# Two attention pipelines: VectorE and ScalarE issued in the written order of the steps, with the steps cut anew

## The chip, the cores and the metric

The program runs on one core of a Trainium2 chip. The metric is the device time of one execution in microseconds (us), as the median of ten runs. A core has five engines that run side by side and wait for one another through semaphores: TensorE (matmuls and transposes; PE in the profile, with its weight loads apart as PEld), VectorE (DVE), ScalarE (ACT), GpSimd (POOL) and SyncE (SP, which here only starts DMAs). Matmul results land in PSUM, a small memory of eight banks per partition; everything else is in SBUF.

## The reference, cut to what matters

The reference is a two-layer decoder over 16 samples of 256 tokens with 256 features, and a context of 120 tokens per sample. Each sublayer is `x = x + f(layernorm(x))`:

- layer 0: causal self-attention with rotary positions (16 heads of 16), cross-attention to the context, and a feed-forward part that picks 10 of 16384 experts for each of 8 heads;
- layer 1: self-attention with a small band added to the scores, a cross-attention whose result is joined as `[c, c2q, c*c2q, c*q2c]` and multiplied by one matrix, and a mixture of 8 experts of which each token uses two.

What the change touches are the two stretches of attention: both attentions of layer 0, and the band attention of layer 1 with the cross-attention and the routing that follow it.

## The kernel before, in words

All 16 samples of `x` stay in SBUF (`xt`), and each stage updates them in place. There are four stretches of time: (1) self- and cross-attention of layer 0 as one pipeline over 32 units (16 samples of the first layer, then 16 of the second); (2) the many-expert part; (3) the band attention of layer 1, beside which the "flow" of each finished sample runs (cross-attention and routing); (4) the mixture of experts, over tiles of 256 tokens.

**The pipeline.** An `Attention` layer has six stages for a unit: `prepare` (layernorm and projections), `ready` (transposed keys and queries), `maxima` (the scores once, for the maximum of each row), `weigh` (the scores again with the maximum in them, and Exp), `values` and `finish`. `run` makes one visit per `v`, and in visit `v` stage `i` works on unit `v - i`. The stages are generators, and each `yield` ends a step. `maxima` and `weigh` go in pairs: at each of their yields they hand out a list of matmuls and a function `after` with what has to be done to the result. `run` issues the two lists in turns, then both `after` functions, then some steps of the other stages (`others_go`: 2 for each pair in the self-attention, 3 in the cross-attention and in stretch 3), then the next pair. A self-attention visit has six pairs, a cross-attention visit four, a band visit eight. The scores of `maxima` have one PSUM buffer (`sa`), so the matmuls of the next pair can't start before VectorE has reduced the last one; the scores of `weigh` have one too (`sb`), which ScalarE empties with Exp. The small results of all other steps go through two rings of two PSUM banks, `t1` and `t2`.

**The order within a visit.** The other stages take turns through `turns`: the first step of `prepare`, the first of `ready`, of `values`, of `finish`, then the second of each, and so on. A visit begins with two of these steps, so TensorE's first work in a visit is the first step of `prepare`. In stretch 3 a second generator, `side`, alternates with them. It begins a new flow in each visit and gives each live flow one step in each of 7 rounds, the older flow first. A flow has 15 steps.

**The layernorm.** `fresh` gives the normalized sample. For the first of each four samples it first takes the statistics of all four (eight tiles, each one BN_STATS and one BN_AGGR on VectorE, lines 119 and 120), the root on ScalarE (line 122), and the reciprocal on VectorE (123). Then, for every sample, `normalized` computes `xn` on VectorE (line 108), and `transposed` turns it on TensorE (131) and copies it to SBUF on ScalarE (132). These last three are in one step. A flow calls `fresh` for its own sample alone, and takes statistics a second time before the routing (lines 1053 to 1057).

**What sets the order of instructions.** In `run` only TensorE stands under `tc.manual_schedule`: its instructions are issued in the order in which the program writes them. For VectorE, ScalarE and GpSimd a scheduler decides at compile time: it goes by the program's order too, but takes a later instruction first where its model finds the earlier one not ready. At run time each engine keeps to the list that came out. ScalarE's functions need tables: a change between the square root and Exp shows as an instruction ACT_TABLE_LOAD.

Lines to follow in the code: `xn` 108; statistics 119 to 123; `run` 165 to 192; maxima 293 (without a mask) and 297, 307 to 309 (causal); Exp 335; the flow 949 to 1158, with its `both` at 1018, its result `y` at 1043, the routing at 1078 to 1137; `side` 1163 to 1171.

Of the kernel before, what the change touches and what calls it, by code (L numbers as in the profile page):

```python
# [13 lines left out]
AF = mybir.ActivationFunctionType  # L14
ALU = mybir.AluOpType
AX = mybir.AxisListType
PSUM = bass.MemoryType.PSUM

P = 128
D = 256  # L20
# [31 lines left out]
def tile_decoder(ctx: ExitStack, tc: tile.TileContext, a: dict, out: bass.AP, last: int = 4):  # L52
    nc = tc.nc
    B = a["x"].shape[0]
# [15 lines left out]
    xt = []  # L70
# [12 lines left out]
    eps = T(cst, [P, 1], "eps")  # L83
    nc.vector.memset(eps, EPS)
    mv = T(cst, [P, NT, 2], "mv")
    rstd = T(cst, [P, NT], "rstd")

    def col(c, n=1):
# [4 lines left out]


    def layernorm_stats(wk):
        for i in range(NT):
            st = T(wk, [P, 6], "bnst")
            nc.vector.bn_stats(st, xt[i // 2][:, i % 2, :])
            nc.vector.bn_aggr(mv[:, i, :], st)
        std = T(wk, [P, NT], "std")  # L100
        nc.scalar.activation(std, mv[:, :, 1], AF.Sqrt, bias=eps)
        nc.vector.reciprocal(rstd, std)

    def normalized(wk, b):
        xn = T(wk, [P, 2, D], "xn")
# [4 lines left out]
            )  # L110
        return xn

    def fresh(wk, b, group=4):

        if b % group == 0:
            ts = range(2 * b, 2 * (b + group))
            for i in ts:
                st = T(wk, [P, 6], "bnst")
                nc.vector.bn_stats(st, xt[i // 2][:, i % 2, :])
                nc.vector.bn_aggr(mv[:, i, :], st)  # L120
            std = T(wk, [P, 2 * group], "std")
            nc.scalar.activation(std, mv[:, ts.start : ts.stop, 1], AF.Sqrt, bias=eps)
            nc.vector.reciprocal(rstd[:, ts.start : ts.stop], std)
        return normalized(wk, b)

    def transposed(ps, xn, dst):

# [30 lines left out]
    def run(stages, n, gap, joint=(2, 3), side=None, more=0):  # L158

        with tc.manual_schedule(engines={mybir.EngineType.PE}):
            for v in range(n + len(stages) - 1 + more):
                going = {i: stage(v - i) for i, stage in enumerate(stages) if 0 <= v - i < n}
                pairs = [going.pop(i) for i in joint if i in going]
                others = deque([turns(going.values())] + ([] if side is None else [side(v)]))

                def others_go(k):
                    while k and others:
                        g = others.popleft()
                        if next(g, 0) is None:
                            others.append(g)
                            k -= 1

                def advance():
                    held = []
                    for g in pairs:  # L180
                        step = next(g, 0)
                        while step is None:
                            others_go(1)
                            step = next(g, 0)
                        if step != 0:
                            held.append(step)
                    return held

                others_go(2)
                held = advance()  # L190
                while held:
                    others_go(gap(v))
                    for pair in zip_longest(*(mms for mms, _ in held)):
                        for mm in pair:
                            if mm is not None:
                                mm()
                    for _, after in held:
                        after()
                    held = advance()
                others_go(-1)  # L200
# [245 lines left out]
    with ExitStack() as st:  # L446
# [21 lines left out]
        half = DH // 2  # L468

        def self_prepare(b, c):  # L470
            xnT = T(wk, [P, 2, S], "xnT")
            transposed(ps, fresh(wk, b), xnT)
            yield
            k, q, v = c["k"], c["q"], c["v"] = ks[b % 2], qs[b % 4], vs[b % 5]
            for t in range(2):
                ts = slice(t * P, (t + 1) * P)
                pp = T(ps, [P, 2 * NH, 2, half], "t1")
                project_rows(pp.rearrange("p h s d -> p (h s d)"), xnT, ts, wa, 0, 2 * D)
                ra = T(wk, [P, 2 * NH, 2, half], "ra", bufs=1)
# [26 lines left out]
            nc.scalar.copy(v[:, :, :, 0:DH], pv.rearrange("p t (h d) -> p t h d", h=NH))  # L506
            yield
# [4 lines left out]
        def cross_prepare(b, c):  # L512
            cT = T(wk, [P, 2, NQ], "cT")
            nc.sync.dma_start(cT, a["ctxT"][b].rearrange("(c p) q -> p c q", p=P))
            xnT = T(wk, [P, 2, S], "xnT")
            transposed(ps, fresh(wk, b), xnT)
            yield
            q, v = c["q"], c["v"] = qs[(b + B) % 4], vs[(b + B) % 5]
            pq = T(ps, [P, 2, D], "t1")
# [325 lines left out]
    with ExitStack() as st:  # L845
# [16 lines left out]
        ps2 = pool(s6, "sc4", 1, PSUM)  # L862

        def band_prepare(b, c):
            c["xnT"] = T(wk4, [P, 2, S], "xnT", bufs=4)
            transposed(ps, fresh(wk4, b), c["xnT"])
            yield

        def band_ready(b, c):
# [78 lines left out]
        def flow(b):  # L948
            load(b)
            cx, cT = context.pop(b)  # L950
            xn = fresh(wk, b, 1)
            nc.gpsimd.tensor_tensor(xt[b], xt[b], badd.unsqueeze(1).to_broadcast([P, 2, D]), ALU.add)

            qc = T(wk, [P, 2, NQ], "qc")
# [20 lines left out]
            for t in range(2):  # L975
                nc.scalar.activation(
                    e[:, t], p_s[:, t], AF.Exp, bias=nm[:, t : t + 1], accum_out=z[:, t : t + 1]
                )
            nc.vector.reciprocal(z, z)
            for t in range(2):  # L980
                nc.scalar.activation(e[:, t], e[:, t], AF.Copy, scale=z[:, t : t + 1])
            yield

            pm = T(ps, [1, 2, P], "t1")
            for t in range(2):
# [3 lines left out]
            be = T(wk, [1, 2, P], "be", bufs=1)  # L989
            bz = T(wk, [1, 1], "bz")  # L990
            nc.scalar.activation(be, pm, AF.Exp, bias=low, scale=-1.0, accum_out=bz)
            nc.vector.reciprocal(bz, bz)
            yield
            pt = T(ps, [NQ, 2, P], "t1")
            for t in range(2):
                nc.tensor.transpose(pt[:, t, :], e[:, t], ident)
# [32 lines left out]
                    )  # L1029
            q2c = T(wk, [P, 2], "q2c")  # L1030
            nc.scalar.copy(q2c, pd)

            wb = T(wk, [P, 2, D], "wb", bufs=1)
            for dc in range(2):
                nc.vector.scalar_tensor_tensor(
                    wb[:, dc, :], wl[:, 6 + dc, :], q2c[:, dc : dc + 1], wl[:, dc, :], ALU.mult, ALU.add
                )
            yield
            parts = [(u, w, c) for u, w in ((att, wl[:, 2:4]), (both, wl[:, 4:6]), (xnT, wb)) for c in range(2)]
            for t in range(2):  # L1040
                y = T(ps, [P, D], "t2")
# [4 lines left out]
                nc.vector.tensor_add(xt[b][:, t, :], xt[b][:, t, :], y)  # L1046
                if t == 0:
                    yield
            xr = T(wk, [P, 2, RW], "xr")
            ts = slice(2 * b, 2 * b + 2)  # L1050
            for t in range(2):
                stats = T(wk, [P, 6], "bnst")
                nc.vector.bn_stats(stats, xt[b][:, t, :])
                nc.vector.bn_aggr(mv[:, 2 * b + t, :], stats)
            std = T(wk, [P, 2], "std2")
            nc.scalar.activation(std, mv[:, ts, 1], AF.Sqrt, bias=eps)
            nc.vector.reciprocal(rstd[:, ts], std)
            shift = T(wk, [P, 2], "shift")
            nc.vector.scalar_tensor_tensor(shift, mv[:, ts, 0], -1.0, rstd[:, ts], ALU.mult, ALU.mult)
            for t in range(2):  # L1060
# [17 lines left out]
            nc.vector.tensor_reduce(red, pl, AX.X, ALU.max)  # L1078
            nc.vector.tensor_tensor(rw, pl, over(red), ALU.subtract)
            nc.scalar.activation(rw, rw, AF.Exp)  # L1080
            nc.vector.tensor_reduce(red, rw, AX.X, ALU.add)
            nc.vector.reciprocal(red, red)
            nc.vector.tensor_tensor(rw, rw, over(red), ALU.mult)
# [51 lines left out]
            for t in range(2):  # L1135
                for k in range(2):
# [5 lines left out]
                    )  # L1142
                    tc.declare_no_dep(ins.ins, group="rows", reason="no two tokens have one place")
                    tc.add_to_no_dep_group("rows", ins.ins)
            yield

            pt = T(ps, [NE, 2, P], "t1")
            for t in range(2):
# [13 lines left out]
        def side(v):  # L1162
            b = v - len(layer.stages())
            if 0 <= b < B:
                flows.append(flow(b))
            for _ in range(7):
                for g in list(flows):
                    if next(g, 0) is None:
                        yield
                    else:  # L1170
                        flows.remove(g)
# [247 lines left out]
```

## Time and profile before

| What | Value |
|---|---|
| median of 10 runs | 3883.72 us (3875.56 to 3890.93) |
| the profiled execution | 3893.37 us, its span 3891.7 us |
| stretch 1, both attentions of layer 0 | from the start to about 752 us |
| stretch 2, many experts | to about 2317 us |
| stretch 3, band attention, flows and routing | to about 3300 us |
| stretch 4, mixture of experts | to the end |
| ScalarE's table loads in stretch 1 at lines 122 and 335 | 5 and 5 |
| table loads from 2290 to 3300 us at lines 335, 122, 1056 | 27, 17 and 16, of 1283 ns each |

The profile names an operation by the line of the program, the engine and the tiles that it writes and reads. "PE sa<-kT,qT" is the score matmul of `maxima`, "DVE q<-sa" its reduction. The answers by time stretch give busy microseconds and, behind them, the clock that was granted to TensorE as a share of full speed. In a list of instructions in order of time, a bracket says how long the engine had been idle before the line and which instruction ended that.

### The profile page before, as it was taken

To read this page: it belongs to the slowest core of one execution; us is meant where nothing else is said; L and a number is where in the kernel's file an instruction comes from. 1 tells how busy PE (TensorE), PEld (TensorE's weight loads), DVE (VectorE), ACT (ScalarE), POOL (GpSimd) and SP (SyncE) were. 2 spreads that over 40 slices of the span, in tenths; PEclk is the share of its full clock that TensorE was granted. 3 is DMA by queue.
4 is the path that set the end of the run, shared out by engine and by line. 5 is a ranking of instruction groups with operands and counts; after the bars stand their busy time and mean duration, and the time that the engine had idled before them with its cause. 6 is when DMAs were issued, how large, how long until landed. Compare 5 with 4: busy or idle time off the path is not lost.

```text
span 3891.7 us, 131086 instructions
## 1 busy us (share of the span) xinstructions
PE 3468.0 (89%) x57482; PEld 2887.7 (74%) x57482; DVE 2295.4 (59%) x9263; ACT 1648.3 (42%) x2873; POOL 1625.9 (42%) x1611
## 2 busy tenths in 40 slices
PE   6999999659999999999999997888888886999999
PEld 4666788458888888888888885666666665788887
DVE  6777543498888888888888733444344433111111
ACT  2555566334444444444444323555454432233222
POOL 2333200036666666666666652333233321333332
PEclk8999999869999999999999997899898866999999
DMA  9200000200000000000000010000000001566564
GB/s 333 92 2 2 5 9 8 94 3 4 4 4 4 4 4 4 4 4 4 4 4 4 4 33 1 4 20 21 17 23 18 22 21 55 170 187 186 172 184 133
DMA packets 49327, 182.01 MB, mean 47 GB/s; under 512 B 14889, under 2 KB 36785, under 8 KB 42354
## 3 DMA queue, kind: packets, MB, share of 16 engines
q1 hardware_dynamic: 29840, 144.22, 10.5%
q0 software_dynamic: 18048, 29.14, 3.6%
q8 instruction: 451, 7.39, 0.8%
q14 instruction: 122, 1.00, 0.1%
q10 hardware_dynamic: 866, 0.26, 0.0%
HBM read 150.66 MB, written 57.15 MB: 53 GB/s over the span
## 4 chain that ended last, share of the span: by engine, by line
PE 67%; DVE 22%; ACT 5%; POOL 3%; issue 2%; DMA 0%; another core or an unknown queue 0%; POOLq 0%; DVEq 0%; ACTq 0%
PE acc L784 9%; PE t L145 7%; PE h L137 7%; PE hid L137 7%; PE y L1283 7%; PE sa L263 6%; DVE hot L740 5%; PE t L759 5%; PE t L368 4%; POOL hot L747 2%; PE t L1043 2%; PE t L137 2%; DVE q L293 2%; PE t L245 2%; PE sb L263 2%
## 5 line engine op out<-in xcount | busy, mean ns | idle before, releaser
L747 POOL TENSOR_TENSOR hot<-hot,w 104x1024 f32<-104x1024 f32 x256 | 523.4, 2045 | 281.4 <-DVE hot L740 177.3
L740 DVE TENSOR_TENSOR hot<-wij,iota 104x1024 f32<-104x1024 f32 x512 | 598.7, 1211 | 61.8 <-ACT w L730 54.0
L137 PE MATMUL hid<-xnT,w_dn 128*128 128x128 f32 x4096 | 522.2, 281 | 3.6 <-issue 2.0
L137 PEld LDWEIGHTS hid<-xnT,w_dn 128*128 128x128 f32 x4096 | 482.7, 193 | 15.2 <-issue 3.4
L784 PE MATMUL acc<-w_up,hg 128*128 128x256 f32 x2048 | 482.1, 381 | 0.0
L263 PE MATMUL sa<-kT,qT 32*128 32x256 f32 (+2 forms) x3072 | 382.2, 371 | 110.1 <-DVE q L293 80.6
L778 POOL TENSOR_TENSOR hg<-hg,gate 128x512 f32<-128x512 f32 x256 | 342.6, 1338 | 255.4 <-ACT hg L777 245.9
L759 PEld LDWEIGHTS t<-hot,hot 104*32 104x32 f32 x32768 | 310.4, 110 | 162.4 <-POOL hot L747 108.7
L759 PE MATMUL t<-hot,hot 104*32 104x32 f32 x32768 | 341.3, 199 | 94.7 <-POOL hot L747 83.8
L335 ACT ACTIVATE pT<-sb 128x1024 f32<-128x1024 f32 (+1 forms) x288 | 295.2, 1025 | 285.2 <-PE sb L263 223.7
L263 PEld LDWEIGHTS sa<-kT,qT 32*128 32x128 f32 x3072 | 257.0, 200 | 201.9 <-DVE q L293 113.2
L784 PEld LDWEIGHTS acc<-w_up,hg 128*128 128x128 f32 x2048 | 371.9, 190 | 42.6
L263 PE MATMUL sb<-qmT,kT 32*128 32x256 f32 (+2 forms) x2560 | 370.0, 412 | 15.2 <-ACT pT L335 15.1
L766 ACT COPY gate<-t 128x512 f32<-128x512 f32 x256 | 271.0, 1058 | 253.2 <-PE t L759 253.0
L293 DVE TENSOR_REDUCE q<-sa 128x4 f32<-128x1024 f32 (+1 forms) x192 | 230.7, 1202 | 182.4 <-PE sb L263 103.1
L346 POOL TENSOR_TENSOR pT<-pT,bandf 128x260 f32<-128x260 f32 x256 | 184.6, 743 | 324.2 <-ACT pT L335 322.1
L137 PE MATMUL h<-xT,wt 128*128 128x256 f32 x1248 | 279.5, 382 | 6.0 <-ACT xT L1274 6.0
L777 ACT ACTIVATE hg<-hid 128x512 f32<-128x512 f32 x256 | 153.7, 601 | 306.1 <-PE hid L137 304.8
L1283 PE MATMUL y<-wt,hT 128*128 128x256 f32 x1248 | 275.7, 379 | 0.0
L137 PEld LDWEIGHTS h<-xT,wt 128*128 128x128 f32 x1248 | 223.9, 190 | 55.3 <-ACT xT L1274 10.8
L1292 POOL DMA_INDIRECT out_y<-ys,toi x78 | 123.4, 1581 | 337.1 <-DVE ys L1291 302.6
L1283 PEld LDWEIGHTS y<-wt,hT 128*128 128x128 f32 x1248 | 237.1, 190 | 32.2
(289 smaller groups left out, 5931.6 us busy)
## 6 DMA issues: line engine op xcount, KB each, us to landing
wt<-in_m_w SPq DMA_DIRECT2D x39, 2052.0 KB, 8.6
rows<-in_zeros SPq DMA_DIRECT2D x32, 1040.0 KB, 28.4
x<-in_x SPq DMA_DIRECT2D x16, 256.0 KB, 4.5
w_dn<-in_p_dn SPq DMA_DIRECT2D x2, 2048.0 KB
w_up<-in_p_up SPq DMA_DIRECT2D x1, 4096.0 KB, 23.6
out_y<-x SPq DMA_DIRECT2D x16, 256.0 KB, 2.1
cT<-in_ctxT SPq DMA_DIRECT2D x32, 120.0 KB, 2.1
cx<-in_ctx SPq DMA_DIRECT2D x16, 120.0 KB, 2.3
```

Of the source, the lines that this page charges most:

```text
L137: nc.tensor.matmul(o, lhsT=w[:, dc, c0 : c0 + n], rhs=rhs[:, dc, :], start=dc == 0, stop=stop and dc == 1)
L145: nc.tensor.matmul(o, lhsT=xT[:, dc, tok], rhs=w[:, dc, c0 : c0 + n], start=bias is None and dc == 0, stop=dc == 1)
L263: nc.tensor.matmul(sc[0 : ls.stop - ls.start, r, g, 0 : rs.stop - rs.start], lhsT=lhs[rows_, g0 + g, ls], rhs=rhs[rows_, g0 + g, rs], star ...
L293: nc.vector.tensor_reduce(to, sc[:, :, :, 0:nk], AX.X, ALU.max)
L335: nc.scalar.activation(pT[0:kn], sc[0:kn], AF.Exp, scale=1.0 / math.sqrt(DH))
L740: nc.vector.tensor_tensor(t, wij[:, k, cs].unsqueeze(2).to_broadcast([HS, NC, PK]), iota[0:HS].unsqueeze(1).to_broadcast([HS, NC, PK]), AL ...
L747: nc.gpsimd.tensor_tensor(hot[1], hot[1], w[:, cs].unsqueeze(2).to_broadcast([HS, NC, PK]), ALU.mult)
L759: nc.tensor.matmul(pg[q * NLO : (q + 1) * NLO, t, :], lhsT=hi[:, t, i0 : i0 + NLO], rhs=hj[:, t, j0 : j0 + NLO], start=True, stop=True,)
L766: nc.scalar.copy(gate[:, :, c * NC : (c + 1) * NC].rearrange("p l t -> p t l"), pg)
L778: nc.gpsimd.tensor_tensor(hg, hg, gate[:, s * L : (s + 1) * L, :], ALU.mult)
L784: nc.tensor.matmul(acc, lhsT=hg[:, i, :], rhs=w_up[:, l, :], start=l == 0, stop=l == NLO - 1)
L1283: nc.tensor.matmul(y, lhsT=hT[:, fc, h * P : (h + 1) * P], rhs=w2[:, fc, :], start=fc == 0, stop=fc == FF // P - 1,)
```

## The change

Five things are done. First, in `run` VectorE and ScalarE join TensorE in the written order. Second, `fresh` becomes a generator: at the first of a group of samples it issues statistics and the root, yields, and issues the reciprocal in the next step; `normalized` is then called by its user, in the same step as `transposed`. Third, the flow's steps are cut differently: the yields stand behind an instruction on ScalarE (or another engine) whose result VectorE reads next. The flow has 17 steps in place of 15. Fourth, `side` gives nine rounds in a visit in place of seven, so that a flow lives for two visits and not for three. Fifth, `std` is one tile for the whole program. No arithmetic is added or dropped.

```diff
+IN_ORDER = {mybir.EngineType.PE, mybir.EngineType.DVE, mybir.EngineType.Activation}
...
+    def stats(wk, b, n=1):
+        ts = slice(2 * b, 2 * (b + n))
+        for i in range(ts.start, ts.stop):
+            st = T(wk, [P, 6], "bnst")
+            nc.vector.bn_stats(st, xt[i // 2][:, i % 2, :])
+            nc.vector.bn_aggr(mv[:, i, :], st)
+        nc.scalar.activation(std[:, ts], mv[:, ts, 1], AF.Sqrt, bias=eps)
+
+    def rstds(b, n=1):
+        nc.vector.reciprocal(rstd[:, 2 * b : 2 * (b + n)], std[:, 2 * b : 2 * (b + n)])
+
     def fresh(wk, b, group=4):
         if b % group == 0:
...
-        return normalized(wk, b)
+            stats(wk, b, group)
+            yield
+            rstds(b, group)
...
-        with tc.manual_schedule(engines={mybir.EngineType.PE}):
+        with tc.manual_schedule(engines=IN_ORDER):
...
         def self_prepare(b, c):
+            yield from fresh(wk, b)
             xnT = T(wk, [P, 2, S], "xnT")
-            transposed(ps, fresh(wk, b), xnT)
+            transposed(ps, normalized(wk, b), xnT)
             yield
...
         def flow(b):
             load(b)
             cx, cT = context.pop(b)
-            xn = fresh(wk, b, 1)
+            yield from fresh(wk, b, 1)
+            xn = normalized(wk, b)
...
                     e[:, t], p_s[:, t], AF.Exp, bias=nm[:, t : t + 1], accum_out=z[:, t : t + 1]
                 )
+            yield
             nc.vector.reciprocal(z, z)
             for t in range(2):
                 nc.scalar.activation(e[:, t], e[:, t], AF.Copy, scale=z[:, t : t + 1])
-            yield
...
             nc.scalar.activation(be, pm, AF.Exp, bias=low, scale=-1.0, accum_out=bz)
+            yield
             nc.vector.reciprocal(bz, bz)
-            yield
...
             nc.scalar.copy(q2c, pd)
+            yield
             wb = T(wk, [P, 2, D], "wb", bufs=1)
...
-            yield
             parts = [(u, w, c) for u, w in ((att, wl[:, 2:4]), (both, wl[:, 4:6]), (xnT, wb)) for c in range(2)]
...
                 if t == 0:
                     yield
+            stats(wk, b)
+            yield
+            rstds(b)
...
             nc.scalar.activation(rw, rw, AF.Exp)
+            yield
             nc.vector.tensor_reduce(red, rw, AX.X, ALU.add)
...
                     tc.add_to_no_dep_group("rows", ins.ins)
-            yield
             pt = T(ps, [NE, 2, P], "t1")
...
-            for _ in range(7):
+            for _ in range(9):
```

`cross_prepare` and `band_prepare` change as `self_prepare` does.

More of the change, by code (lines that the diff above doesn't have):

```diff
@@ L85, in tile_decoder @@
     mv = T(cst, [P, NT, 2], "mv")
+    std = T(cst, [P, NT], "std")
     rstd = T(cst, [P, NT], "rstd")
@@ L95, in layernorm_stats @@
     def layernorm_stats(wk):
[L96 to L102, printed above, removed]
+        stats(wk, 0, B)
+        rstds(0, B)
     def normalized(wk, b):
@@ L111, in normalized @@
         return xn
+    def stats(wk, b, n=1):
[7 more added lines that the diff above has]
+        nc.vector.reciprocal(rstd[:, 2 * b : 2 * (b + n)], std[:, 2 * b : 2 * (b + n)])
     def fresh(wk, b, group=4):
         if b % group == 0:
[L116 to L123, printed above, removed]
-        return normalized(wk, b)
+            stats(wk, b, group)
+            yield
+            rstds(b, group)
     def transposed(ps, xn, dst):
@@ L514, in cross_prepare @@
             nc.sync.dma_start(cT, a["ctxT"][b].rearrange("(c p) q -> p c q", p=P))
+            yield from fresh(wk, b)
             xnT = T(wk, [P, 2, S], "xnT")
-            transposed(ps, fresh(wk, b), xnT)
+            transposed(ps, normalized(wk, b), xnT)
             yield
@@ L864, in band_prepare @@
         def band_prepare(b, c):
+            yield from fresh(wk4, b)
             c["xnT"] = T(wk4, [P, 2, S], "xnT", bufs=4)
-            transposed(ps, fresh(wk4, b), c["xnT"])
+            transposed(ps, normalized(wk4, b), c["xnT"])
             yield
@@ L1048, in flow @@
                     yield
+            stats(wk, b)
+            yield
+            rstds(b)
             xr = T(wk, [P, 2, RW], "xr")
             ts = slice(2 * b, 2 * b + 2)
[L1051 to L1057, printed above, removed]
             shift = T(wk, [P, 2], "shift")
```

## The prediction

> **What bounds the kernel now.** I read the page first, then busy time and granted clock by stretches, then the instructions in order of time where one visit ends and the next begins, then TensorE's waits.
>
> ```profile
> PE 3468.0 (89%) x57482; PEld 2887.7 (74%) x57482; DVE 2295.4 (59%) x9263; ACT 1648.3 (42%) x2873; POOL 1625.9 (42%) x1611
> PE   6999999659999999999999997888888886999999
> PEclk8999999869999999999999997899898866999999
> ```
>
> TensorE bounds every stretch. The change touches slices 1 to 8 (stretch 1) and 24 to 33 (stretch 3); the second group has the idle time and the low clock. By stretches (busy us, and after POOL the clock):
>
> ```profile
> 100.00:400.00 300.00, 273.06 (x3533) 197.51 (x3532) 229.90 (x529) 155.31 (x228) 96.90 (x137) 0.99 0.08 28
> 500.00:700.00 200.00, 194.14 (x2614) 166.24 (x2612) 81.99 (x134) 130.75 (x269) 13.02 (x19) 1.00 0.03 8
> 2609.00:3051.70 442.70, 384.44 (x3365) 289.85 (x3365) 197.60 (x559) 221.85 (x410) 149.72 (x206) 0.90 0.06 20
> ```
>
> Self- and cross-attention leave 9% and 3% of TensorE idle, at full clock. The third line is eight visits of the band (from one square-root table load of line 122, at 2609.07 us, to the eighth after it, at 3051.7): 55.3 us each, of which 58.3 / 8 = 7.3 us idle, and 10% of the busy time, 4.8 us, lost to the clock. What little there is to win is there. TensorE's waits from 2460 to 3180 us say on whom:
>
> ```profile
> PE sa L263 <- DVE q L293: 43.6, 27, 3.6
> PE t L1149 <- ACT batt L1004: 14.3, 6, 3.1
> PE sb L263 <- ACT pT L335: 10.2, 11, 1.1
> PE t L1111 <- DVE either L1102: 8.0, 10, 0.9
> ```
>
> The lines that decide are those of a visit's end. In the self-attention, TensorE:
>
> ```profile
> 265.81 0.37 PE L263 MATMUL sb<-qmT,kT 32*128 32x256 f32 x1
> 266.11 0.65 PE L131 MATMUL t<-ident,xn 128*128 128x128 f32 x4
> 266.60 0.60 PE L245 MATMUL t<-ident,k 128*128 128x128 f32 x4
> 267.83 0.66 PE L245 MATMUL t<-ident,q 128*128 128x128 f32 x4 [0.62 <-ACT xnT L132]
> ```
>
> and VectorE:
>
> ```profile
> 266.23 0.76 DVE L297 TENSOR_TENSOR own<-sa,causal 128x256 f32<-128x256 f32 x2
> ...
> 267.50 0.68 DVE L308 TENSOR_REDUCE m<-own 128x4 f32<-128x512 f32 x1
> 268.09 0.40 DVE L108 TENSOR_SCALAR xn<-x,mv,rstd 128x256 f32<-128x256 f32 x1
> ```
>
> The last score matmul ends at 266.2, and line 131 follows without a gap: it turns an `xn` that VectorE made a visit earlier. The `xn` at 268.09 belongs to the next visit's sample. VectorE runs ahead, because the scheduler let it. In the cross-attention it is the same: line 131 starts at 552.14, right behind the scores, while VectorE reduces them until 553.4 and only then makes the next `xn`:
>
> ```profile
> 552.34 1.16 DVE L293 TENSOR_REDUCE q<-sa 128x8 f32<-128x960 f32 x1 [1.34 <-PE sa L263]
> 553.41 0.73 DVE L108 TENSOR_SCALAR xn<-x,mv,rstd 128x256 f32<-128x256 f32 x2
> ```
>
> **What the change does to the head of a visit.** `normalized` and `transposed` stay in one step, and it is the first of the visit. In the written order `xn` stands behind the reduction of the last pair, and TensorE, in the same order, has nothing in front of line 131. So the run-ahead is lost.
>
> Self-attention, samples that don't begin a group: the maximum's chain takes VectorE to 268.3, two `xn` (0.73) to 269.1, and line 131 starts there in place of 266.11: 3.0 us. It absorbs the 0.62 us wait for `xnT` shown above (the Exp before it on ScalarE is then over). Net 2.4 us. Visits 3, 5 to 7, 9 to 11, 13 to 15, 17 and 18: 12 x 2.4 = 29 us.
>
> Cross-attention: 553.41 + 0.73 + 0.05 - 552.14 = 2.05 us. Visits 19, 21 to 23, 25 to 27, 29 to 31: 10 x 2.05 = 20.5 us. What queues behind line 131 on TensorE (line 137, 1.9 us) can't cover it, for it comes later in the order.
>
> **Groups.** At the first of four samples the first step is eight statistics, and ScalarE's root behind them stops everything that follows on ScalarE. At the end of stretch 1 the same pair of instructions comes every 0.68 us:
>
> ```profile
> 752.04 0.43 DVE L98 BATCH_NORM_STATS2 bnst<-x 128x6 f32<-128x256 f32 x1
> 752.51 0.18 DVE L99 BATCH_NORM_AGGREGATE mv<-bnst 128x2 f32<-128x6 f32 x1
> 752.72 0.43 DVE L98 BATCH_NORM_STATS2 bnst<-x 128x6 f32<-128x256 f32 x1
> ```
>
> Eight are 5.4 us. Counted from 266.2: maximum to 268.3, statistics to 273.7, root (0.30) to 274.05, then the copy of `kT` (0.59) that frees a `t1` bank, 274.65. TensorE has the turned keys, the first turned queries and the sums (0.5 + 0.5 + 1.5) and is out of work at 268.7: 6.0 us. Today the four groups of the self-attention take their statistics before 28 us, beside the load of `x`, so visits 4, 8 and 12 pay all of it: 18 us. For the cross-attention the same count gives 6.0 at visit 16 and 4.4 at 20, 24 and 28 (shorter maximum, 1.9 us of line 137 as cover): 19.2. Today's four cost 2.24, 2.24, 2.5 and 1.4 us of TensorE (the stalls behind the loads at 213, 313, 407 and 494): +10.8. At the start the first copy of `xnT` no longer stands behind the fourth root (27.20): TensorE begins at 26.7 and not at 28.13, -1.4.
>
> Waits in stretch 1: 29 + 20.5 + 18 + 10.8 - 1.4 = +77 us.
>
> **The clock.** One of today's stalls, in order of time,
>
> ```profile
> 218.18 1.05 PE L245 MATMUL t<-ident,q 128*128 128x128 f32 x4 [2.24 <-ACT xnT L132]
> ```
>
> (the last bracket is the stall), by stretches:
>
> ```profile
> 215.00:218.00 3.00, 0.95 (x8) 0.71 (x7) 2.65 (x8) 2.95 (x4) 0.28 (x1) 1.00 0.00 0
> 218.00:221.50 3.50, 3.32 (x48) 2.83 (x52) 0.51 (x1) 1.21 (x3) 0.36 (x1) 0.54 0.02 5
> ```
>
> A stall of 2.24 us was followed by 3.4 us at half clock: 1.7 us of TensorE's work lost. A stall of 1.46 us, at 2622 us, had no such stretch behind it; I take 1.5 us within one clock period of 3.4 us as the point. A stall of 3 us always meets it: 12 x 1.7 = 20. One of 2.05 us does so from 72% of its places: 10 x 0.72 x 1.7 = 12. The groups' 4 to 6 us empty two periods: 7 x 3.4 - 4 x 1.7 = 17. Together +49 us; the ends are 0 and, with three periods as after 450 us, 150.
>
> The Trainium skill, "TensorE: Matmul & The Clock Gate", in the part on HAM oscillation, has as its rule to leave no idle gap over about 3.4 us. By the rule stalls of 2 to 3 us would cost no clock, and the groups' term alone, 17, would be left in place of 49. The row at 218 us says otherwise, so I go by the row.
>
> **Stretch 3.** What goes: VectorE's inversions. At 2610.13 a reduction stood 3 us behind routing work of line 1102 to 1125 that its matmuls had overtaken; in the written order it comes first. Line 1111 no longer waits for `either`, made a step earlier. Of the table loads, the flow's two roots now lie in the second and third of `side`'s steps, both ahead of the first pair, so a visit has one change to the root and one back, in place of two each (2.6 us less on ScalarE). I leave 1.5 us of today's 7.3 idle. What comes: line 131 behind the eighth reduction and `xn`, 1.28 + 0.8 = 2.1 us; and the new flow's line 131 behind the older flow's second `y`, for VectorE must add (0.43), take two statistics (1.36) and make `xn` (0.8) with only `aoT` (0.25) on TensorE between: 2.4 us. So idle 6.0 in place of 7.3. Clock: 0.72 and 0.85 of 1.7 = 2.7 in place of 4.8. Gain 3.4 us a visit, for 13 visits (6 to 18) 44 us. Against it: groups at visits 8 and 12, 3.8 + 1.7 more each, 11; visits 3 and 5 (no flows yet), 4; visit 4, 6. Visits 16 to 18 have no `prepare`: -6. Net -29 us. Ends: a gain of 7.6 a visit (idle only the two new stalls, full clock), -99; or the old waits stay and the new ones come on top, 7.2 a visit, +94. I take the middle because each removed wait can be named and so can each new one. After visit 18 only flows run, chains that no order shortens: 30.4 us a visit today by the table loads of line 1056 (3184.2, 3213.8, 3245.8); I put 0, within 10 us either way.
>
> No instruction of GpSimd's or SyncE's is moved by hand; a flow's two loads of context stay at its first step, a step before their first use. Stretches 2 and 4: 0. They start when the pipelines end.
>
> Sum: 77 + 49 - 29 = +97. The profiled execution, 3893.4, would become 3990; it lies 9.7 us above the median, so 3884 + 97 = 3981 us.
>
> **Rivals.**
>
> *The clock repays it (not slower).* Single stalls between full periods cost no clock, and in the band, where today's come in clusters (0.78 and 1.34 us within 3), it stays full: -99 there with 15 back for the groups and the early visits, +77 in stretch 1, about -7: 3877. For it: 1.46 us at 2622 had no half-clock stretch behind it. Against it: 218 us. It decides from 77 / 13 = 6 us gained per band visit on. Chance 0.18, two thirds to three quarters of it faster.
>
> *The band loses too.* Its waits stay and ScalarE, blocked by the roots, adds the new ones: 77 + 49 + 94 = +220, 4104. For it: ScalarE's idle time before the roots of lines 122 and 1056 is already 30 and 48 us there. Against it: the loads halve. Chance 0.13.
>
> *The change doesn't do what it says*: the issue order on VectorE stays as it is at the heads, and little moves: 3884. Against it: TensorE follows the written order under the same call. Chance 0.04.
>
> **How the numbers follow.** My forecast has 0.65, its own range +30 to +150 (clock 0 and band -47, to both at their bad side): 3914 to 4034. For 8 in 10 the range must reach into both large rivals: 3865 to 4085 leaves out about half of each. Faster by over 0.2% (8 us, about what a measurement of this kernel tells from none): 0.14 from the first rival. Same: 0.04 + 0.04. Slower: 0.65 + 0.13 = 0.78.
>
> **What would show it.** In the waits, "PE t L131" (by its new number) on `xn`: some 22 times 2 to 3 us in stretch 1, once or twice a visit in stretch 3. Statistics in runs of eight with a root and a long wait of ScalarE behind them, seven times. Clock from 100 to 750 us below 0.95. Table loads in stretch 3: some 40 in place of 67. If line 131 still follows the scores without a gap, the prediction is wrong; if it waits but the clock stays at 0.99, it is wrong by half.

## The result, and the profile after

| | before | after |
|---|---|---|
| median | 3884.14 us (28 runs) | 3985.31 us (8 runs) |
| ratio | 1 | 1.0262, 95% interval 1.0248 to 1.0275 |
| profiled execution, its span | 3893.37, 3891.7 us | 3983.08, 3981.4 us |

The changed kernel is 2.6% slower: 3985 us where 3981 was predicted. First the page of the changed kernel (busy time and share of the span, then tenths in 40 slices):

```profile
PE 3498.1 (88%) x57482; PEld 2914.6 (73%) x57482; DVE 2314.5 (58%) x9263; ACT 1620.9 (41%) x2851; POOL 1624.0 (41%) x1611
PE   6888888865999999999999998788888988899999
PEclk8999989977999999999999998898888976899999
```

TensorE was at 9 in the second to seventh slice and is at 8 in the second to eighth; the clock's digits say little here, for 9 covers all from 0.9 up. The same stretches as in the prediction (busy us, then the granted clock, the third line again eight visits of the band):

```profile
100.00:400.00 300.00, 248.48 (x3006) 179.50 (x3007) 202.55 (x463) 136.95 (x198) 79.51 (x115) 0.93 0.09 29
500.00:700.00 200.00, 176.61 (x2176) 148.89 (x2175) 74.68 (x142) 110.85 (x218) 17.40 (x24) 0.91 0.03 7
2709.50:3129.07 419.57, 376.03 (x3371) 290.40 (x3370) 210.83 (x578) 200.71 (x395) 153.56 (x208) 0.88 0.07 21
```

The idle share of TensorE went from 9% to 17% in the self-attention and from 3% to 12% in the cross-attention, and the clock from 0.99 and 1.00 to 0.93 and 0.91. Eight band visits take 419.6 us, 52.4 each, where they took 55.3.

In the table below, and in all that follow, "idle" is the sum of the gaps of over 0.05 us between TensorE's matmuls, and "half" the time in which the clock records show half speed. While TensorE works in such time, half of it is lost. Where a sum below takes half of a difference in "half", it is an estimate, for TensorE also stands idle in part of it (in stretch 1 it works through 80 of the 85.8 us that came on top). Stretch 1 is counted here from 28 us to the first `wij` of the many-expert part, stretch 2 from there to the last `hid` matmul, stretch 3 on to the first gather of rows, and stretch 4 to the end.

| | stretch 1 | idle | half | stretch 3 | idle | half | table loads, stretch 3 |
|---|---|---|---|---|---|---|---|
| before | 786.8 | 98.9 | 101.6 | 994.5 | 161.0 | 335.7 | 67 |
| after | 895.2 | 165.4 | 187.4 | 970.4 | 146.2 | 330.3 | 39 |

Stretch 1 lost 108 us: 66.5 of idle time, and 85.8 us more at half clock, worth 43. Stretch 3 won 24. Stretches 2 and 4 went from 1495.8 to 1500.3 and from 586.5 to 587.4. The sum of the four, 89.7, is the difference of the two profiled executions, 3983.1 - 3893.4; the medians are 101 apart because the profiled execution of before lay 9 us above its median and that of after 2 us below. Comparisons with its stretches hold to some 10 us.

A head of a visit in the self-attention, changed kernel, in order of time (line numbers are now 134 for the transposes and 105 for `xn`):

```profile
270.24 0.68 DVE L310 TENSOR_REDUCE m<-sa 128x4 f32<-128x512 f32 x1
...
270.84 0.67 DVE L311 TENSOR_REDUCE m<-own 128x4 f32<-128x512 f32 x1
271.54 0.17 DVE L312 TENSOR_TENSOR q<-m 128x4 f32<-128x4 f32 x1
271.62 0.73 DVE L105 TENSOR_SCALAR xn<-x,mv,rstd 128x256 f32<-128x256 f32 x2
...
272.09 1.22 PE L134 MATMUL t<-ident,xn 128*128 128x128 f32 x4 [2.57 <-DVE xn L105]
```

VectorE goes through the whole maximum and only then makes `xn`; TensorE, which has nothing else in front of line 134, stands for 2.57 us. In the kernel before there was no gap at this place. What it costs behind that, by stretches of 3.5 us (the number after POOL's is the clock):

```profile
272.40:275.90 3.50, 3.50 (x30) 2.86 (x33) 0.00 (x0) 1.76 (x3) 0.00 (x0) 0.50 0.02 5
275.90:279.40 3.50, 3.50 (x44) 2.71 (x37) 0.00 (x0) 1.27 (x3) 0.15 (x1) 0.65 0.00 0
```

And the head of a group of four samples, visit 12:

```profile
332.60 0.39 DVE L115 BATCH_NORM_STATS2 bnst<-x 128x6 f32<-128x256 f32 x1
333.03 0.18 DVE L116 BATCH_NORM_AGGREGATE mv<-bnst 128x2 f32<-128x6 f32 x1
333.25 0.30 ACT L117 ACTIVATE std<-mv,eps 128x8 f32<-128x8 f32 x1 [4.06 <-DVE mv L116]
333.45 0.56 ACT L253 COPY kT<-t 128x512 f32<-128x512 f32 x1
...
334.07 1.12 PE L248 MATMUL t<-ident,q 128*128 128x128 f32 x4 [3.91 <-ACT kT L253]
```

The root stops ScalarE for 4.06 us until the eighth statistic is made; the copy of `kT` stands behind it, and TensorE waits 3.91 us for the bank which that copy frees. All of stretch 1, as TensorE's waits from 28 to 850 us (total us, times, longest):

```profile
PE t L134 <- DVE xn L105: 46.6, 23, 2.6
PE sa L266 <- DVE m L310: 19.3, 20, 1.6
PE t L248 <- ACT kT L253: 15.6, 4, 3.9
...
PE t L248 <- ACT kT L538: 10.5, 3, 3.5
```

Lines one, three and four are new: 12 stalls of 2.56 to 2.65 us, nine of 1.66 or 1.67 and two of 0.3 on `xn`, and seven on `kT` at the groups.

In stretch 3 the change moved the waits. TensorE's before (2300 to 3300 us):

```profile
PE sa L263 <- DVE q L293: 68.5, 46, 3.6
PE t L1111 <- DVE either L1102: 15.3, 14, 2.7
PE t L1149 <- ACT batt L1004: 15.0, 9, 3.1
```

and after, where the stretch lies some 100 us later (2400 to 3400 us):

```profile
PE t L134 <- DVE xn L105: 53.8, 35, 3.4
PE sa L266 <- DVE q L296: 33.0, 26, 1.4
PE t L1115 <- DVE either L1106: 9.7, 5, 2.8
PE t L1050 <- DVE wb L1043: 8.3, 2, 4.6
```

`q` was halved, `either` lost a third and `batt` is gone; `xn` came instead.

### The profile page after: what moved, and what is told of

It is laid out like the page before. It is cut to its first block, busy times and chain, and to the rows that moved or that the text cites. A ratio compares the mean times of both kernels' runs of the same rounds, so it can differ in the third digit from the quotient of the medians.

```text
span 3981.4 us, 131064 instructions
## 1 busy us (share of the span) xinstructions
PE 3498.1 (88%) x57482; PEld 2914.6 (73%) x57482; DVE 2314.5 (58%) x9263; ACT 1620.9 (41%) x2851; POOL 1624.0 (41%) x1611
## 4 chain that ended last, share of the span: by engine, by line
PE 66%; DVE 25%; POOL 3%; ACT 2%; issue 2%; DMA 0%; POOLq 0%; ACTq 0%; DVEq 0%
PE acc L789 8%; PE t L148 7%; PE sa L266 7%; PE h L140 7%; DVE hot L745 7%; PE y L1286 7%; PE hid L140 6%; PE t L764 4%; PE t L371 3%; PE t L140 3%; PE t L1050 2%; DVE q L296 2%; POOL hot L752 2%; PE t L248 2%; PE sb L266 2%
## 5 line engine op out<-in xcount | busy, mean ns | idle before, releaser
L266 PE MATMUL sa<-kT,qT 32*128 32x256 f32 (+2 forms) x3072 | 367.8, 365 | 74.3 <-DVE q L296 43.1
L266 PE MATMUL sb<-qmT,kT 32*128 32x256 f32 (+2 forms) x2560 | 360.3, 405 | 7.2 <-ACT pT L338 7.2
```

Source lines behind the costliest of these rows:

```text
L266: nc.tensor.matmul(sc[0 : ls.stop - ls.start, r, g, 0 : rs.stop - rs.start], lhsT=lhs[rows_, g0 + g, ls], rhs=rhs[rows_, g0 + g, rs], star ...
```

## The experiments

Three questions were open. Do the waits for `xn`, and the clock behind them, make all of stretch 1's loss? Which engine's order makes it? And is the gain in stretch 3 that of the written order, as I had argued, or that of the new cut of the steps?

The table shows the engines in the written order (P = TensorE, V = VectorE, A = ScalarE), the median, the ratio to the kernel before on the same chip with its interval, and stretches 1 and 3 of the profiled execution as above. The first eight ran on two chips on which the kernel before took 3882 us (e1 to e4) and 3886 us (e5 to e8). The last four ran on two other chips on which it took 3841 and 3842 us; their times are compared with one another only within one set, and with the others by ratio or by idle time, and even a ratio may not carry over in full, for the clock differs. The profiled execution of e5 lay 19 us above its median; the excess is in stretch 4 (607.7 us where all others have 585.7 to 587.5), so its stretches 1 and 3 can be compared.

| | order | median | ratio | stretch 1 | idle | half | stretch 3 | idle | half |
|---|---|---|---|---|---|---|---|---|---|
| before | P | 3884 | 1 | 786.8 | 98.9 | 101.6 | 994.5 | 161.0 | 335.7 |
| after | PVA | 3985 | 1.0262 (1.0248 to 1.0275) | 895.2 | 165.4 | 187.4 | 970.4 | 146.2 | 330.3 |
| e1 | PVA | 3862.6 | 0.9951 (0.9935 to 0.9968) | 810.4 | 120.9 | 98.7 | 932.5 | 132.6 | 236.5 |
| e2 | PA | 3804.3 | 0.9801 (0.9784 to 0.9817) | 778.8 | 94.3 | 97.6 | 909.9 | 111.5 | 257.1 |
| e3 | PV | 3972.8 | 1.0237 (1.0219 to 1.0254) | 882.8 | 162.2 | 166.9 | 973.2 | 147.3 | 337.7 |
| e4 | P | 3840.4 | 0.9890 (0.9866 to 0.9914) | 785.9 | 95.7 | 112.9 | 947.0 | 142.7 | 274.7 |
| e5 | PVA | 3822.7 | 0.9832 (0.9816 to 0.9849) | 779.4 | 97.3 | 78.2 | 925.4 | 128.4 | 233.2 |
| e6 | PVA | 3823.6 | 0.9836 (0.9820 to 0.9853) | 779.7 | 96.7 | 71.4 | 930.3 | 103.5 | 306.7 |
| e7, old steps | PA | 3976.9 | 1.0227 (1.0210 to 1.0244) | 812.6 | 116.0 | 125.2 | 1052.5 | 209.1 | 363.5 |
| e8, old steps | P | 3883.4 | 0.9997 (0.9988 to 1.0007) | 787.7 | 98.9 | 109.2 | 978.6 | 134.1 | 340.6 |
| e9 | PVA | 3802.2 | 0.9898 (0.9869 to 0.9926) | 779.5 | 97.2 | 74.8 | 905.7 | 118.2 | 215.5 |
| e10 | PVA | 3800.9 | 0.9903 (0.9871 to 0.9935) | 792.6 | 112.4 | 78.2 | 890.0 | 104.9 | 219.5 |
| e11 | PA | 3776.0 | 0.9831 (0.9803 to 0.9860) | 774.5 | 92.0 | 77.0 | 892.4 | 110.1 | 220.8 |
| e12 | P | 3825.3 | 0.9963 (0.9949 to 0.9976) | 780.2 | 95.1 | 98.2 | 934.0 | 140.4 | 248.5 |

### e1: `xn` one step before its transposes

In `self_prepare`, and alike in `cross_prepare` and `band_prepare`:

```diff
             yield from fresh(wk, b)
+            xn = normalized(wk, b)
+            yield
             xnT = T(wk, [P, 2, S], "xnT")
-            transposed(ps, normalized(wk, b), xnT)
+            transposed(ps, xn, xnT)
```

> The changed kernel with one more yield in the three prepare functions, between normalized (xn on VectorE) and transposed (its use on TensorE). Theory H (xn in the step of its use stands behind the last reduction of the visit before, and the clock falls after each such stall): in stretch 1 the 46.6 us that TensorE waits for xn go, and with them about 24 x 0.8 half-clock periods of 3.4 us, some 30 us of work; in stretch 3 about 13 waits of 2.1 us and 15 us of clock. 3985 - 47 - 30 - 27 - 15 = 3866; I say 3850 to 3910. Rival A (ScalarE's fixed order with its roots and copies is what holds the pipeline; xn is only what is named last): the wait moves to the next copy, 3955 or more. Rival B (the stalls are real but the clock had its low time from the groups alone): 3985 - 47 - 27 = 3911 or more.

Measured: 3862.6 us, 123 below the changed kernel. In stretch 1 the wait for `xn` is gone from the list, which now begins (TensorE's waits, 28 to 800 us):

```profile
PE t L248 <- ACT kT L253: 15.9, 5, 3.9
PE sa L266 <- DVE m L310: 13.9, 15, 1.6
PE sa L266 <- DVE own L300: 11.1, 17, 0.9
PE t L371 <- POOL pT L341: 11.1, 13, 0.9
PE t L248 <- ACT kT L542: 10.5, 3, 3.5
```

Stretch 1 is 84.8 us shorter: 44.5 of idle time, as the 46.6 of the wait, and 88.7 less at half clock, 44 us of work. So the same 46.6 us cost about twice that, and the half-clock time in the changed kernel is put down to those stalls by taking them away. What is left over before, 24 us, is the groups' 26, which e1 did not touch. Stretch 3 gained another 38.

### e5: also the statistics of a group ahead of it

`moments` is the statistics alone, without the root; each `prepare`, in its last step (in the band in the step of its transposes), makes those of the sample four later, so that the root of a group finds all four made.

```diff
-    def stats(wk, b, n=1):
+    def moments(wk, b, n=1):
...
+    def stats(wk, b, n=1, known=False):
+        if not known:
+            moments(wk, b, n)
...
-            yield from fresh(wk, b)
+            yield from fresh(wk, b, known=b > 0)
             xn = normalized(wk, b)
             yield
...
+            moments(wk, (b + 4) % B)
```

> The kernel with xn a step ahead (3862.6), and the statistics of a group no longer in one burst: each prepare takes those of the sample four later in its last step, so that the root finds them made. H: the cost of the groups goes: in stretch 1 some 20 of the 24 us that still lie above the time before the change (810 against 787), in stretch 3 some 8; 3825 to 3845. Rival E (the groups cost by the root's table loads on ScalarE, which stay): 3855 or more.

Measured: 3822.7 us. Stretch 1 is 31 us shorter than in e1 (idle 23.6 less), and with 779.4 us below the 786.8 of the kernel before. `xn` (85) and the groups (31) together are 116 us: all of the 108 that the change had cost in stretch 1, and 7 more.

### e2 and e3: ScalarE alone, VectorE alone

```diff
-IN_ORDER = {mybir.EngineType.PE, mybir.EngineType.DVE, mybir.EngineType.Activation}
+IN_ORDER = {mybir.EngineType.PE, mybir.EngineType.Activation}
```

> The changed kernel with TensorE and ScalarE in written order, VectorE left to the scheduler. H: VectorE runs ahead again, xn and the statistics are there when asked for, the root no longer waits for eight statistics: stretch 1 within 15 us of the time before the change; stretch 3 keeps the halved table loads. 3865 to 3900. Rival A: the cost stays, 3950 or more.

```diff
-IN_ORDER = {mybir.EngineType.PE, mybir.EngineType.DVE, mybir.EngineType.Activation}
+IN_ORDER = {mybir.EngineType.PE, mybir.EngineType.DVE}
```

> The changed kernel with TensorE and VectorE in written order, ScalarE left to the scheduler. H: the waits for xn stay (47 us and some 30 us of clock in stretch 1); the groups' part (26 us of waits for kT behind the root, 17 us of clock) shrinks, because the copies can go ahead of the root. 3930 to 3970. Rival A: near the time before, 3900 or less.

Measured: e2 3804.3 us, e3 3972.8. VectorE's order is more than the whole loss: it alone stands between e2 and the changed kernel, 181 us, 116 of them in stretch 1 and 60 in stretch 3. e3 came out 3 us above what I expected; without ScalarE's order the groups' stall stays and is merely booked on `xn` (TensorE's waits of e3, 28 to 800 us):

```profile
PE t L134 <- DVE xn L105: 72.0, 30, 3.6
```

These are 30 stalls where the changed kernel had 23 on `xn` and seven on `kT`. e2 was far better than I expected (3865 to 3900), which opened the question of the next runs: 78 us below the kernel before must come from the steps themselves, or from ScalarE's order.

### e4: the new steps, only TensorE in order

```diff
-IN_ORDER = {mybir.EngineType.PE, mybir.EngineType.DVE, mybir.EngineType.Activation}
+IN_ORDER = {mybir.EngineType.PE}
```

> The changed kernel with only TensorE in written order, as before the change: the new cut of the steps and the nine rounds alone. H: the steps matter little without the order: 3870 to 3900. Rival C (the new cut, 17 steps in nine rounds, is what makes it slower, or what gains 23 us in stretch 3): 3930 or more, or 3865 and less.

Measured: 3840.4 us, 42 below the kernel before, against my expectation. Stretch 1 is as before (785.9 against 786.8); the gain is in stretch 3, 47.5 us: 18 of idle time and 61 at half clock. So the new steps gain with no written order on VectorE or ScalarE. Whether they do it through TensorE's order or through the lists of the other engines, for which the scheduler starts from the new steps too, is not separated here. The table loads are 63 where they were 67, so they can have little part in it.

### e7: the old steps with ScalarE in order

```diff
-        with tc.manual_schedule(engines={mybir.EngineType.PE}):
+        with tc.manual_schedule(engines={mybir.EngineType.PE, mybir.EngineType.Activation}):
```

> The kernel before the change with TensorE and ScalarE in written order, its old steps and seven rounds kept. With the new steps ScalarE's order was worth 36 us (3840 to 3804). Theory S (the order alone does it): 3840 to 3860. Theory C (it needs the new cut, for in the old steps ScalarE waits in order for what VectorE has just been asked): 3880 or more.

Measured: 3976.9 us. ScalarE's order costs 91 us with the old steps (3976.9 against 3885.8 in the same set) and wins 36 with the new ones (e4 to e2). TensorE's waits of e7, from 2400 to 3200 us, show the place:

```profile
PE t L131 <- DVE xn L108: 47.4, 15, 3.5
PE t L1149 <- ACT batt L1004: 21.6, 8, 3.2
```

Neither is in the list of e2. In the old steps the statistics, the root, the reciprocal, `xn` and its transposes are one step; once ScalarE may not take the root early, TensorE waits for the whole chain. The new steps put a yield behind the root. So ScalarE's order pays only with the new cut of the steps; that of all its yields it is the one behind the root that counts is read from these waits, and no run has that one alone.

### e8: the old steps with a flow in two visits

```diff
-            for _ in range(7):
+            for _ in range(8):
```

> The kernel before the change with eight rounds in side in place of seven, nothing else: a flow of 15 steps then lives for two visits, not three. The new steps with the old order gained 42 us. If two live flows in place of three are what gains: 3840 to 3855. If it is the place of the cuts: 3875 or more.

Measured: no difference, 3883.4 us. Stretch 3 is 16 us shorter in the profiled execution, with 27 us less idle time and as much time at half clock, but the medians don't show it. That a flow lives for two visits is not the cause of e4's gain.

### e12: the routing half of the new cut undone

```diff
             nc.scalar.activation(rw, rw, AF.Exp)
-            yield
             nc.vector.tensor_reduce(red, rw, AX.X, ALU.add)
...
+            yield
             pt = T(ps, [NE, 2, P], "t1")
```

> The steps of e4 with only the routing half of the flow cut as before (the yield behind the Exp of the routing goes back to the place ahead of the turned weights); TensorE alone in the written order. The cross-attention half, the root in a step of its own and the nine rounds stay. e4 was 0.989 of the kernel before, and stretch 3 was 947 us in place of 994.5. Between those two, TensorE's wait at the routing's transposes for the copy of batt fell from 15.0 us to none and its wait for either from 15.3 to 5.5. Theory (the gain of the new cut is the routing's): most of it goes, the ratio is 0.994 to 1.000 and stretch 3 is over 970 us. Rival (the gain is that of the cross-attention half and the root's step): the ratio stays at 0.987 to 0.992, stretch 3 below 960 us.

Measured: ratio 0.9963 in place of e4's 0.9890. By the ratio the theory holds: two thirds of the gain gone. By the trace it doesn't: stretch 3 has 140.4 us idle, e4 had 142.7, and it is 934 us long, below the 960 of the rival. The waits moved (TensorE's of e12, 2300 to 3300 us):

```profile
PE t L1114 <- DVE either L1105: 14.5, 8, 2.7
...
PE t L1152 <- ACT aT L1005: 8.1, 8, 1.2
...
PE t L1030 <- ACT batt L1011: 3.0, 2, 1.5
```

`either` is back at 14.5 (5.5 in e4) as the theory wanted; `batt` is not, for its 3.0 us stand at another line and stood there in e4 too. This ran on a chip where the kernel before took 3842 us, and no profile of that kernel was taken there, so its own half-clock time is not known. Which yield carries e4's 42 us stays open; one profile of each, on two chips, speaks against the routing's for the idle part, 18 us.

### e6 and e9: the flow's `xn` ahead as well

e5 still waits in stretch 3, from 2300 to 3200 us:

```profile
PE sa L271 <- DVE q L301: 32.0, 25, 1.4
PE t L139 <- DVE xn L105: 23.7, 14, 2.1
PE t L1066 <- DVE wb L1059: 20.1, 18, 2.1
```

e6 puts a yield between the flow's `normalized` and its `transposed`, which makes 18 steps:

```diff
             xn = normalized(wk, b)
+            yield
...
             transposed(ps, xn, xnT)
```

> The same, and in the flow a yield between normalized and transposed, so that a new flow's transposes no longer stand behind the older flow's second y, its statistics and xn (18 steps in nine rounds). H (the second new stall of the prediction, 2.4 us in 13 visits and the clock behind it): 25 to 45 us less than the statistics-ahead kernel, 3785 to 3815. Rival D (in stretch 3 VectorE's order costs by other chains, wb before y above all: 22.8 us of waits there): less than 12 us.

Measured: 3823.6 us, the same as e5, where 3785 to 3815 was expected. The waits for `xn` and `wb` are gone and stretch 3 is 25 us less idle, but 73 us more of it are at half clock, for which I have no cause that a run shows. The run tells less than it was meant to: with 18 steps the roots of the older and the newer flow no longer fall in neighbouring steps, and the table loads rose from 39 to 63. e9, again from e5, keeps 17 steps by joining the transposes to the step that follows:

```diff
+            yield
             xnT = T(wk, [P, 2, S], "xnT")
             transposed(ps, xn, xnT)
-            yield
```

> This is the kernel of e5 with the flow's third step cut behind the normalization and not behind the transposes of it: the flow keeps 17 steps, so the two roots of the older and the newer flow stay side by side (39 table loads in stretch 3, not 63 as in e6). Theory (a stall in the flow's head is a stall like any other): the 25 us that TensorE waits for xn in stretch 3 of e5 and 10 to 20 us of half-clock work go, stretch 3 becomes some 890 to 900 us in place of 925, the whole 3780 to 3800. Rival (as e6: a wait taken away at this place comes back elsewhere or as half clock): stretch 3 stays above 915, the whole 3812 or more.

Measured: 3802.2 us, ratio 0.9898, on a chip where the kernel before took 3841. The table loads stay at 39. The wait for `xn` went from 23.7 to 3.7 us, but idle time in stretch 3 fell by 10 only: `wb` kept 17.1 and a new wait came (TensorE's of e9, 2300 to 3200 us):

```profile
PE t L1066 <- DVE wb L1059: 17.1, 17, 1.4
PE t L987 <- ACT kT L905: 8.0, 9, 1.4
```

More than half of the idle time that the theory wanted was handed on to the next instructions in the list. Stretch 3 is 20 us shorter than in e5, but e9's ratio is above e5's 0.9832; the two did not run on one chip, so whether e9 beats e5 is open.

### e10 and e11: can the run-ahead be written back?

e10 makes `xn` a whole visit ahead by hand: the last step of each `prepare` issues the statistics, root, reciprocal and `xn` for the next unit.

```diff
-            yield from fresh(wk, b, known=b > 0)
-            xn = normalized(wk, b)
-            yield
+            if b == 0:
+                yield from first(wk)
...
-            transposed(ps, xn, xnT)
+            transposed(ps, made.pop(b), xnT)
...
+            yield from ahead(wk, (b + 1) % B, b + 1, 2 * B)
```

> The kernel of e9 with xn written a whole visit ahead: each prepare ends with the normalization for the next unit (and, before a group, its statistics, root and reciprocal), so that the written order of VectorE has the run-ahead that the scheduler gave it. Theory (what VectorE's written order lost is the run-ahead, and it can be written back): nothing in a visit's head is waited for, no xn waits of TensorE are left in stretches 1 and 3, 5 to 30 us less than e9, 3760 to 3795, level with or below the 3804 of e2. Rival (the scheduler's order is better because it also fills other gaps, or the band's xn is not the bound): not below e9, and above 3804.

e11 is e9 with VectorE given back to the scheduler:

```diff
-IN_ORDER = {mybir.EngineType.PE, mybir.EngineType.DVE, mybir.EngineType.Activation}
+IN_ORDER = {mybir.EngineType.PE, mybir.EngineType.Activation}
```

> The kernel of e9 with VectorE given back to the scheduler (TensorE and ScalarE in the written order, as in e2). If VectorE's written order costs time only through the waits for xn, which e9 takes away, e11 is within 10 us of e9, and the cut of the flow brings nothing beyond e2: 3785 to 3805. If the scheduler's order for VectorE has more to give than the run-ahead of xn, e11 is 15 us or more below e9 and below e2: under 3785.

Measured in one set, on one chip: e9 3802.2, e10 3800.9, e11 3776.0. In e10 stretch 3 gains 16 us (`wb` falls from 17.1 to 3.3) and stretch 1 loses 13, where TensorE now waits for maxima that stand behind the added work (`m` 16.2 to 23.2 us), for `xnT` (8.3 us) and, against the theory, still for `xn` (4.2 us where e9 had 0.4). The rival holds for the sum: no gain. The scheduler's order is 26 us better than the written one even in e9, where hardly any `xn` is waited for (0.4 us in stretch 1, 3.7 in stretch 3): 5 us in stretch 1 and 13 in stretch 3 of the profiled executions. Another 11 us lie in stretch 2, where the orders are not written by hand in either; I have no cause for these.

The best versions are e2 (2.0% below the kernel before) and e11 (1.7%). They ran on different chips, and their intervals overlap; e11's idle time in stretches 1 and 3 is 202 us, e2's 206. The simplest of them, e2, is the changed kernel with one engine's name taken out.

## Why the prediction came out right, and which step did not

**Stretch 1 was right by its steps.**

| | predicted | measured |
|---|---|---|
| self-attention, `xn` | 12 x 2.4 = 29 | 12 of 2.56 to 2.65, 31 |
| cross-attention, `xn` | 10 x 2.05 = 20.5 | 9 of 1.66 or 1.67, 15 |
| groups | 6.0 at four, 4.4 at three: 37 | 3.91 at four, 3.50 at three: 26 |
| waits in all, less today's 8.4 and the start | 77 | idle time +66.5 |
| clock | 49 | half-clock time +85.8, worth 43 |
| stretch 1 | 126 | 108 |

The mechanism and the places are those of the prediction, and the count but for one: in visit 19 TensorE has scores to go through until 519.4 us, and `xn` is made by 518.5. The cross-attention's term was 0.4 us a visit too large. In the groups I took the pair of statistics at the 0.68 us of today's trace, where they run while other work fills VectorE's list; eight in a row came every 0.53 us (from 328.88 us to 333.1), 1.2 us less for the eight. Another 0.85 us of the stall stands a little earlier, ahead of line 371, as a wait for `pT`, so that each of the four costs 4.76 us in all.

**The clock, by the row and not by the rule.** In the changed kernel's stretch 1, 14 of 15 stalls of 1.5 to 2 us and 11 of 12 of 2.5 to 3 us have more than 1 us at half clock in the 6.8 us behind them, 4.1 and 3.7 us on average; so have 6 of 12 of 1 to 1.5 us. So the point that I took, 1.5 us, was near enough, though it is no sharp one, and the 72% for the shorter stalls too low. That the stalls bring the half clock, and do not only stand ahead of it, is shown by e1. The Trainium skill, "TensorE: Matmul & The Clock Gate", in the part on HAM oscillation, sets the limit for an idle gap at about 3.4 us; here stalls of half that length cost clock, and e1, in which those on `xn` are gone from stretch 1, has 88.7 us less at half clock.

**Stretch 3 was right in its sum and wrong in its cause.** Predicted: 29 us won, a visit of 51.9 us, some 40 table loads. Measured: 24 won, 52.4 us over the eight visits above, 39 loads. The new stalls were predicted at (2.1 + 2.4) x 13 = 58 us and are 53.8 in 35; of the waits that were to go, only part went. The clock's term did not come: 2.1 of the 3.4 us a visit were to be won by it, and the granted clock of the eight visits went from 0.90 to 0.88, the time at half clock in the stretch only from 335.7 to 330.3. In its place TensorE's idle time fell further than forecast, from 7.3 to 5.4 us a visit and not to 6.0, and its busy time by 1 us, which I had not foreseen and have no cause for. Above all, I put the gain down to the written order: "What goes: VectorE's inversions", in the first place. The runs take it apart otherwise (stretch 3, profiled executions):

- the cut of the steps alone: 994.5 to 947.0, a gain of 47.5 (e4);
- ScalarE's order on top: to 909.9, a gain of 37, with the table loads halved (e2);
- VectorE's order on top: to 970.4, a loss of 60 (the changed kernel).

VectorE's order does end its inversions. TensorE's longest wait of e2, 2300 to 3300 us, is

```profile
PE sa L266 <- DVE q L296: 61.5, 38, 2.7
```

and the changed kernel has 33.0 us of it; but for those 28 us VectorE's order brings 53.8 of `xn`, which e2 does not wait for. The step that failed is that one: the inversion was priced as a pure loss of the scheduler's, though it is the same run-ahead whose value I had counted in stretch 1. And the cut, which I gave no price of its own, was worth more than the whole sum for the stretch. That these errors, and the clock's, cancelled is luck; my expectations of e4 and e2, from the same view of the order, missed by 30 and 60 us.

**The rivals.** That the clock repays it is excluded: the time at half clock rose by 86 us in stretch 1 and stayed in stretch 3. That the band loses too is excluded for the change as a whole, but true of VectorE's order alone (60 us). That the order does not change is excluded by the 2.57 us at 272.09.

## What to carry to other kernels

Before an engine is put in a written order, look for what it does earlier today than it is written: here each such instruction that another engine needs at the head of a visit became a wait, and each engine had its own price (VectorE a loss of 181 us, ScalarE a gain of 36). Try the engines one by one, and the new cut of the steps without any of them; a sum that comes out right can hide parts of both signs. In stretch 1 TensorE's stalls of 1.7 to 2.6 us, once in a visit, cost not quite twice their length (46.6 us of them, 84.8 us in all), the rest of it through the clock.

## What the runs showed of the hardware

- The kernel before took 3882 to 3886 us in the sets of e1 to e8, on two chips, and 3841 and 3842 in those of e9 to e12, on two others, 1.1% apart, with a mean clock of about 0.939 and 0.944. Times from different chips can't be compared at the level of a per cent without a run of a common kernel beside them.
- Less idle time need not be less time: e6 has 25 us less of it in stretch 3 than e5 and 73 us more at half clock, and the two take the same time within 1 us.
